# GpSimd's additions wait one VectorE operation earlier, the gating product moves to VectorE, and the second convolution's residual is added from PSUM

## The chip, the cores and the metric

The kernel runs on one core of a Trainium2 chip. The metric is the device time of one execution in microseconds (us), here the median of three runs: 3256.88 us (3255.39 to 3258.67). A difference of about 0.2% (6.5 us) is what the measurement of this kernel can tell from no change.

## The reference, cut to what is computed

Four layers follow each other on an image batch `x` of 4 x 128 channels x 64 x 64.

```
# layer 0: attention over the 4096 pixels, 16-wide queries and keys
attn = softmax(q^T k);  x = gamma * (v attn^T) + x
# layer 1: two 3x3 convolutions with quantised weights, batch norm, 4-bit activations
r  = quant(clip(bn1(conv(x, w1)), 0, 1))          # 15 levels
x  = quant(clip(bn2(conv(r, w2)) + x, 0, 1))      # the residual is added before rounding
# layer 2: a selective scan along the pixels, 256 inner channels, 16 states
xh, z = split(x @ W_in);  xh = silu(causal_conv(xh))
dt, B, C = softplus(...), ...
h[n] = exp(dt * A[n]) * h[n] + dt * B[n] * xh     # a recurrence over 4096 pixels
y  = sum_n h[n] * C[n] + D * xh
y  = y * silu(z)                                  # the gating product
x  = silu(group_norm(y @ W_out)) + x
# layer 3: attention over the pixels, 64-wide; x = x + wo @ agg
```

## The kernel before, in words

Every layer is written as Python generators ("chains"): `energies`, `exponentials` and `products` for the two attentions, `convolutions`, `preparation`, `scans`, `additions`, `output` and so on. Each `yield op(...)` ends a step. The long string `SCORE` has one letter per step (`VOICES` maps letters to chains), and `Order.run` issues the steps in that order. So each engine's program order is written out by hand, across all chains, and is fixed. The costs inside `op(...)` were input to whatever wrote the string and have no effect here; `bank=True` marks a step that takes the one-bank PSUM buffer `gtile` (tag `g`), which a later `release()` gives back.

The pixels of an image are cut into blocks of 512 (the first block of the first image into two of 256), 33 blocks in all. Both halves of the 256 inner channels lie side by side, so a block of one state is 128 partitions x 1024 values. Per block, `preparation` (letter f) makes the inputs, and then for 16 states `m`:

- `scans` (letter n): for every pair of states one VectorE multiplication `hs = ud * b_n` of 2048 values (L1311); for every state two scans of 512 values (L1331), whose decays `da` ScalarE has written to PSUM (L1285); after the next multiplication's scans, `readout` multiplies the pair by `c_n` in place (L1348). On VectorE the steady order is L1311, scan, scan, L1348, scan, scan, L1311 and so on. `hs` has three buffers.
- `additions` (letter o): for every state one GpSimd addition `y += hs` (L1359). After the sixteenth, GpSimd also makes the gating product `y *= sz` (L1363), and `output` (letter g) multiplies by `W_out`.

Which GpSimd operation runs beside which VectorE operation is set by two helpers. `held(inst)` stores the VectorE operation just issued, and `behind(inst)` makes a GpSimd operation wait until the stored one has ended. `held` is put around the VectorE operations that the author calls port operations: L1311, L1348, the four of `preparation` (L1139 to L1148), those of `convolutions` (L938, L950, L977, L984, L987) and L1226. An addition that follows such an operation in the SCORE waits for its end.

The second convolution of `convolutions` (letter e) ends in four steps: ScalarE scales the PSUM bank into an SBUF tile `t` and releases the bank (L973); VectorE adds 15 times the residual image to `t` (L977), clamps it to 0..15 (L984), and rounds it by adding and subtracting a large constant into the FP8 image `x1` (L987).

The attention of the seven first stages runs on TensorE and ScalarE beside the scans. The attention of layer 3 of the last image needs that image's whole layer 2 and runs after the last scan, with VectorE adding the exponentials (L681).

Of the kernel before, what the change touches and what calls it, by code (L numbers as in the profile page):

```python
# [20 lines left out]
P = 128  # L21
W = 64
# [52 lines left out]
    "finish3": "CDEFGHIJ",  # L75
# [4 lines left out]
ittiiuccbvaauitatiaiswjaijaiiukuiviajkajiitkwtiikjijkikcuuisjbbibjkbbittikjjidkikuujiikjibbxcjik  # L80
xxkxbajijabjikkikjjiidxkjayyyykijyieeesejkibjseeiceeceeeekfjkffkijfikffkjjiifdxfjfffxkjxffffpffk
xiixpesfkjkfeffjenlnmlnnfmniinpekfellhmjfnnknenomjoifjkfinhmnlnnmjeifkdlijenpyneylnommjkkihlneyi
eefsnjojknnnflnlhmmffopnnnnfiinkynfkkjiyomlmhjnfpnoonnojlfiknpnjflfmfnonnsmfhkldffnoffkxxnnnxlol
mfppxxnehkfiinenfffejmnnjofekiehlneofmelnjmnnonnikejieneesjflkmeikohjmlnnijpnnijlnophmmnkfflkons
nnodiynijnnyppjmylflfhmkkinjoonnifjfnolflnnnommhnnkfpffkifnnnlnfmhmjokpgonlnnifngjllnfhmfonnnfmn
nikfjffylfmlhpyfmiiokfkdonnonnnnjofkfpfhfknjisljmijfnnonkkploinmnipjjkklnonomnfiikjjhinolkjdfimj
nxnikfxfxxlpnnkxfppjxmoxkkenehenmlijonijeelnmkniijpeeokenhjlnneeeiiemknojnjlfppfnhmkpiodnjinnjfo
kkflkmnnfkflinnmnijhjponppflfmknoniinjogfjklimjgijhnnlkfnokffmndypnpijffnyyfylkkpnyymynflhiejmff
onennokkffijffieejekhkmieelnijnfeenopkinejlmjkndiikjjnloihpneiknjmpnopnklkojpinmfnjikhklnnfomnne
oijflpiknfjkisjfpmdnxjlnmnnoxhpnoiffxjxkkpiljxmiffjnnogklxxmhiisknnojgffkgpennlfefkjifnemopnnejo  # L90
limhiennkjfnpejklnpmfofdiijelnfmkknfnhjoninifjflgnjmnkkijikkjplmpohnifinnonjjkklmnfdijonyffeeffe
ipheenkkjmlnnyykypiiyyojyjffkiijkkknejelopmnnnpmklninhjoiejiipjsdelkjnnompiiknelnhmnffonklnmonnf
fejjkppnfkifpilofmnhnnjjoekflmnzffknnggglpniokotzzzmitudenuxhnelneieeoivmittpfnufuhnmlnpiiwntpit
xxolununxxmfffnflxxmopneheoffffffinnnefeepfelnimtntponeveeesieelomuuniwneefijkhnliifnojjmnijpnln
pkhomiijnneeeejlpkknmnonpkiefelmeeopjnnhfkinijjlmknnkidijmkonlnnfkffsijohljimpnnfjkijkijnoeplenh
pnffmokipljnnoofnfkiimlgnjggkmnknfpnofdyphlnnyfikmfynyoyyjmylpnnonhfnkijjfpfkflmijnonnijlkijkmnn
ophijpkeiiljfkfnmekjonnfpffldmnpoehnnnijiffekifjfpklkjnmnkiikejofnlmphnonnjkiijkjefkofldxnmnijxx
xpnijhlmnkonkiikexjnxxlmonknsijikjjippnlfkjffmennfphijoinlfnmnoefkjlmnhnpopnnofffokidigfkglfmfgp
jnnjhnmfklepoekeiifnnjnpjkelonkimnnpffielojjmkfnffhinijknlonmkdynjeklneepeiyikyyeoyhnmjpnnpyjkif
ylnfoijmkkjneielnihjnkjmiinjjolnmeeeeonnffkfffkpiednppoijjeflkkhnmienenjifkmelpjnokkiijnknjiiljm  # L100
jnhonnklkdmxnpnoijinopjlnkxxxkfmnksxfxpiixhlnnkjmfjofinejnilnjohmnepenoopkfkiiffjlkmffgnkpngeefd
kglnjiiemonhnnepjmoljnkfnfelfkijnfmfnhokifipnnkjipjlmikjfjfkonnnlmfpnfonhkdlnnfeiijmyjeokknlipim
nkpnnojikjhjeenepoilijkjnmnpffiifkffnyyjkyykiydljhmnynkokijifjkklnesjemijonnpnilnmnpfeoekeenpjol
mkiinneknjljepneomkdnxffnepeiijkofxxmfplnxjnkenffxijiopkxxmlknjineljnijpnfkmifonejilkkgmnonnnooj
fgkfmlngeeippnsdelnjmnnpikfoeijfknifjijjfflekkinmonifkfnjklmnnojpffkfnlpiimnonnfjlkndmynjeeioeek
kjlymiyyispenynppkyjjoiikkfjynfffeefnjkfilnjeemneoenkiiljemnkepndkjomlniijhnnpofnkjkilisoenmnjkk
pneofjilmfipjnjhnlnkzfkfmfonnlfpenitkpthimdnxpuxunzxonffiilnvtitxxxiexolzzuumenwimentfitugnounfi
phgngipfgvttfloiggnmniuuoplwffffijnmonghiigjjlnnpknmfnfkoiifeljenmjnnpflhonekepiimfjopnkejlnknii
pkhjmijnjelnonmeeeinoggponffggeffikkfdggkggggggeejglgnjgnkgeeesmgknggeihijkkjlngpgiinokmejknpjlg
nghkpmdnyoiiejjgenijyilkyyykmnegeeynnyfokfijjijkpnkmlnniiheofknjoffjmlnppfinenoijlmknsjfhfnnkoio  # L110
igfdjkjfpmplngkffkgfniglfmhnieefnnjonjiikelekpmoenjnknjlmhoinnpnjifkklfjmopfiidnxnjxnlnmffnjkkox
hfpknpxxxpolmfixnjnijlenphkeomnknijnifjpffkffmiljknknofnpieojeidljhmnnnijeekkkoliijkjmknnnfiflij
jpmhkkeoknnpnildnjmnyioejepnelosypynkiiykyhjmyynkjinijlfkfmjfkffnnpoeeminphoilnkejnffmklnnfjoini
ejlghnjngmnkefoedipnepeoifgslmkfojekknnnpffmeiholjennienkjjemlnfipiojnffkkpnplfhomnjnknieffflkjd
iixnmnonpkjxlxxxnojkxmnxihijjlkefnkkmenonffiifjeeppfjfehknilmknpnionejjijkdlnoijmipnnokkijlifneh
mnnkjjkoeilmeiknkfppnnfjleejsonmnifhniokjjplnfkfmdyinepnijfopljkfyfmkyyhyiinlnfmjnpoyyjneeokgnkk
fgflmgnofhnnfnilimnnjkefpejieiojlmfknnnffhokpnjlmideppiojfkkfjifnnnlnmhjniojlnfmkkiijjkninliksfp
onohmpknnnjjlmokdpnnxfffffnpeikxxxkjijleijmnknhelijoffnexmninkjkijkopnmloijnkhnpnlopkxndmiinxene
jjlnkkiimhnjjkkponepiiflkjknomnenpfjmhfslnnfoknppiijjflkfmfdnynonifljhggmnonnooijikjelyyngyeymne
pikyfyfphlkffnomfnnnelnipofffjmpnjfffehkklnnmenioepneeijlkjnmnoeisijnflkjkidnomhpnneiejjolkfkknm  # L120
nffffkiijefejempepniiplokkhnejnnjezekeflpomknzznnlniimnhvonwliopdxnviminnfwlnfxfimznfhvopenlnfmo
infwxpfifenvhxospmlnnnoofxwlgmingjijpnxxliijgnnmnjhkkkkifofppnikjlkffnmofkipjlfkfnnnhfmnonkfijif
kplnjmokifnnjjkdloidimhjpjennnmelfnkkponkkkknopifjmlhijnfeeijpennfijfflkkkfeokijmnnkkiiddpnjkplj
mehkoiiennnjklpeekknjskmioniCljnhnjiiomnjnfflmnnCkkkokkpjkldpijenifmodhnfnnppjijklomknniienfplkk
fkjmknnhonojklnfiiemknpnjkfjlinhoimnnjppjofkkkfilnmddijnjglengkkkhmnfnonpokfkkflmfpnAiinnjejlehe
mnofnnoijffflmnniiffefkppkjCilkkCChfnCpmnonnooeCkkjjCidCdfgjmklfnnkfffkijijfenhlnkkkminopjepnelo
ikjfCksknDmDniipjkkkenjliioddknjkmpnnpkijlijkjnmkflkiionnmnnjjofkknfplmnnofifjieplnfpfmonnnkjifo
kkojflgfinifpgmkgjfflnmDnonDnnDDDiDjBddilnkkomnDkkklpkmpnojjfnnnfffiljmnifnkkiffoEkEppnjlmonnkkj
pkfflndiijEndikEomjkknknilpEmoEjpiEFjnnnkkkolnFijmnfffjDAffkkinjloiEnEpmfjpnEikknkjiidldmFFkojnn
jnkoklphFmnnnkkiFFiBfjlnFjkkmnFppiiojjlnnkkipjmoinffhknflfnomnkfpjfkdlmhnffioinnnojojlgdgiimnffk  # L130
gppkkjngklggknfpfiomhnjkjnnklnffmiiffnojklkjijmnpfpfFinnAfhofnkkloGGmnnnkddjlnphmofninGGjpplnikk
kkomGkGinGjkjlGmGhijijnnnggpokknfkffkiikfkgjiddlfjkmfHoGnnHnkjlnkoihmpjijnHniiHHkkHHBookflnmpnji
jlgHjmpHnnnohgngkkgggggggpggmgiglkkfkoknnifjfpjggnifidggodlmnfgjkkfnjgkhilgmpnfgpngknoHjfkgkknfo
fiflgfmhnjnifglkgnomjkijfffnlppnmknnionjfkkffpihniddIIlpkmjojIInnhimlnniknpfokjkjnmiiklnfIjnkljk
onphmkkijijnolnniomkppAkkjiIiddIjkknnnlnmnjhfoknpffifIflInijjkkkmnkoiinjjfkklzhmopkknkddnzznittl
noJpiuimulJvinhtInpJtinouuzBiimngJfoJpwntlimtunuJnopnJiolvinmftthniflununpffiomfnwfifjlmnffhngpn
ofglkJnmJijnoffnijlkmhippnnojfijnmknlfffnonijplnhnomnkfkpifjinjfklmiJpjijnkknfdionhlnojippmnjkln
mnkijfionnkjlmikjnknoppffhfnfpijmikjlkfkdnyoinnpijkjijlnikyyyykomynyjiihnkjlefmennjlonmhopkijfkn
neeiienelmjkoppkdijjnnlhmnnokennpkffiiljjonkmffnnpkiljmhionnnpjffikjlmgnfkpfkfnflonmohnnngooikgj
dxffijgmlxikixxxpnkjxknjfxnmlnpipofehjfnneiijkfmpljfinnkojfnfkomlnnfiihnkkjojmlpfdnfnneifffiekkp  # L140
jhmejlfonnneppkiikjijlmjoninneljknkkimikjodnyhlemeneepjenyoyinkyykyijynijkklppnmioneejlhinnjokej
fmfenlpinpneimokjfkffinhnlnojmneijfklnopdmjhnnfifkjnooelnfkfmgkiffigfnmglpkfpenhnnjjlioneeminpjj
kfkfnlonnffpijimnjophneekkldfxonmnfijfnikkxxjiolnmhnixxpknojjlxkxnipimjfnkkfekenlffpfejmeinjlnki
dehjoikffjkknmfenpfopiinneeojlkmihpnnjeiknejjmkipeoljinlnmnknijkjndlhyyyyiioekkmnppyjnjynhloynmk
npofenniijoflkjfpnkmnenifijfjmkpoflhnnijnijfloofkmfnnggkfiihfgdlpkfennjmnfejkeonleomneffflknppni
infkojminjhnoplfinkkjkmnnijliopnfmfnhjplnkdxjnmnoneiexxjliejepekfknoxxkimijxxlenkkeehenfpjffiifk
jkponmnijfnlhmenknijdikofnjlkpijimjennopnlenmkkojheeinnpjmiljpknfonnkiijljkfiknomfnhpjfenedfmyii
lnoknejjyfknfyyyiioyylnppmnkfhnjjelnfmnpofekfgkinglmnniohnffjjmlnnkoepigojieejnelmnfhokfkiniffdj
jefppnlfokfmnnnpkijflnieemkjhfnkiiojneekkejfplffmnkkzzzzndpxiiolvimnxxnnohwfnlviifpxxmownvnnoilp
miwhfnnnivwxxlnpmiiojjiilnnkefkpepnokmnnpolnjjmleeneniikomkjkfkjknnnfifmolnnppejnijlofmnnnoikjkk  # L150
# [37 lines left out]
class Order:  # L188
# [32 lines left out]
    def run(self):  # L221
        for voice in SCORE:
# [7 lines left out]
            if item[1] is None:  # L230
                self.chains.pop(voice)
# [1666 lines left out]
```

## Time and profile before

| what | value |
|---|---|
| median of three runs | 3256.88 us |
| the profiled execution | 3258.73 us |
| its span, first to last instruction | 3256.9 us |
| TensorE busy in the span | 3075.6 us |
| VectorE busy | 2942.3 us |
| ScalarE busy | 2550.4 us |
| GpSimd busy | 1298.7 us |
| mean granted TensorE clock | 0.983 |
| first scan starts, last read-out ends | 104.9 us, 2933.0 us |

The profile has one row per group of instructions (line, engine, operation, shapes, count, busy time, mean duration) and a timeline per engine. Two things help in reading it. A VectorE operation that follows another directly begins, by the record, some 80 ns before the other's recorded end, so the time that one more operation takes up is its duration less 0.08 us. And the duration of an operation holds whatever time it is kept from its operands after its start, so the same operation on the same shape can have different durations; the shortest tenth shows what it takes undisturbed.

### The profile page before, as it was taken

Reading aid. Unit: us, or ns where it says so; the run is one execution under the profiler, and the core shown is the slowest. Engines: PE = TensorE matmul, PEld = TensorE weight load, DVE = VectorE, ACT = ScalarE, POOL = GpSimd, SP = SyncE. Lnnn points to the kernel's source line nnn. Section 1 sums busy time; section 2 is a strip of 40 time slices with the busy share of each in tenths; the row PEclk is TensorE's granted clock in tenths of the full one; section 3 lists DMA queues with packets and bytes.
Section 4 is the critical chain, followed back from the end, with each engine's and each line's share of the span. In section 5 each row is a group of like instructions: output and inputs, shape, how many; then the busy total and the mean of one; then the engine's idle time right before and its main releaser. Section 6 shows DMA issues by size and latency. Waiting matters only on the chain. (4 is left out here: it accounts for less than half of the span.)

```text
span 3256.9 us, 69082 instructions
## 1 busy us (share of the span) xinstructions
PE 3075.6 (94%) x29404; PEld 2260.7 (69%) x29404; DVE 2942.3 (90%) x2377; ACT 2550.4 (78%) x3734; POOL 1298.7 (40%) x582
## 2 busy tenths in 40 slices
PE   8989989999899999999898999999899999999998
PEld 7878858888688887555556878865566555565665
DVE  3699999999999999999999999999999999993554
ACT  5888878888788887888787888878888888875554
POOL 0244444444344444444444444444444444450000
PEclk9999999999999999999999999999999999999999
DMA  2233333233333334333333222233333333330000
GB/s 71 81 99 106 102 118 104 96 108 105 108 117 103 104 102 131 105 109 117 111 130 127 99 98 93 97 125 109 104 125 114 133 114 113 119 108 11 2 11 22
DMA packets 134878, 321.67 MB, mean 99 GB/s; under 512 B 44384, under 2 KB 55072, under 8 KB 134560
## 3 DMA queue, kind: packets, MB, share of 16 engines
q1 hardware_dynamic: 134272, 316.32, 28.9%
q8 instruction: 232, 3.80, 0.5%
q10 hardware_dynamic: 288, 0.85, 0.1%
q14 instruction: 86, 0.70, 0.1%
HBM read 300.35 MB, written 16.78 MB: 97 GB/s over the span
## 5 line engine op out<-in xcount | busy, mean ns | idle before, releaser
L1359 POOL TENSOR_TENSOR y<-y,hs 128x1024 f32<-128x1024 f32 (+1 forms) x528 | 1220.0, 2311 | 1569.1 <-DVE hs L1311 644.6
L659 ACT ACTIVATE p<-e 128x1024 f32<-128x1024 f32 x1024 | 1016.4, 1019 | 183.5 <-PE e L641 161.7
L1331 DVE TENSOR_TENSOR_SCAN hs<-da,hlast,hs 128x512 f32<-128x512 f32 (+1 forms) x928 | 1124.7, 1249 | 36.6 <-ACT da L1285 15.8
L723 PE MATMUL us<-v,p 128*128 128x129 f32 x8192 | 1012.9, 280 | 23.7 <-ACT us L780 11.2
L723 PEld LDWEIGHTS us<-v,p 128*128 128x128 f32 x8192 | 964.5, 194 | 81.4 <-ACT p L659 16.8
L1285 ACT ACTIVATE da<-dt,late 128x512 f32<-128x512 f32 (+1 forms) x1056 | 705.5, 677 | 303.4 <-DVE hs L1331 292.0
L1311 DVE TENSOR_TENSOR hs<-ud,b_n 128x2048 f32<-128x2048 f32 (+1 forms) x264 | 620.0, 2348 | 6.3 <-POOL y L1359 4.2
L1348 DVE TENSOR_TENSOR hs<-hs,c_n 128x2048 f32<-128x2048 f32 (+1 forms) x264 | 590.8, 2238 | 4.5 <-DMA c_n<-bc_d 2.3
L641 PE MATMUL e<-it,v 64*128 64x256 f32 x4096 | 531.6, 396 | 21.7 <-ACT p L659 21.3
L732 PE MATMUL us<-p,v 128*32 128x256 f32 x8192 | 501.8, 383 | 4.7 <-ACT p L659 4.1
L641 PEld LDWEIGHTS e<-it,v 64*128 64x128 f32 x4096 | 373.1, 188 | 162.4 <-issue 74.8
L732 PEld LDWEIGHTS us<-p,v 128*32 128x32 f32 x8192 | 246.2, 110 | 216.5 <-issue 53.3
L641 PE MATMUL e<-it,j 64*128 64x256 f32 x2048 | 208.8, 313 | 24.5 <-ACT p L659 19.3
L641 PEld LDWEIGHTS e<-it,j 64*128 64x128 f32 x2048 | 142.7, 186 | 88.0 <-ACT p L659 31.6
L751 PE MATMUL us<-p,ones 128*32 128x256 f32 x3072 | 202.6, 381 | 0.0
L681 DVE TENSOR_TENSOR acc<-p,acc 128x1024 f32<-128x1024 f32 x96 | 117.5, 1224 | 39.3 <-ACT p L659 32.5
L751 PEld LDWEIGHTS us<-p,ones 128*32 128x32 f32 x3072 | 96.1, 110 | 72.9 <-issue 13.2
L1331 DVE TENSOR_TENSOR_SCAN hs<-da,hs 128x512 f32<-128x512 f32 (+1 forms) x128 | 133.2, 1074 | 7.0 <-ACT da L1285 4.4
L1028 PEld LDWEIGHTS <-w 128*128 128x128 bf16 x594 | 53.1, 98 | 85.8 <-issue 43.9
L1028 PE MATMUL xh<-x,w 128*128 128x512 fp8e4 (+1 forms) x396 | 94.7, 375 | 14.0 <-ACT xc L1074 6.7
L1363 POOL TENSOR_TENSOR y<-y,sz 128x1024 f32<-128x1024 f32 (+1 forms) x33 | 75.9, 2301 | 71.4 <-DVE hs L1348 54.8
L681 DVE TENSOR_TENSOR acc<-p 128x1024 f32<-128x1024 f32 x16 | 19.6, 1224 | 83.1 <-PE ss L694 44.4
(173 smaller groups left out, 2563.6 us busy)
## 6 DMA issues: line engine op xcount, KB each, us to landing
b_n<-bc_d SPq DMA_DIRECT2D x256, 512.0 KB, 3.7
c_n<-bc_d SPq DMA_DIRECT2D x256, 512.0 KB, 3.7
x_in<-in_x SPq DMA_DIRECT2D x16, 512.0 KB, 6.1
xpad<-in_x SPq DMA_DIRECT2D x32, 256.0 KB, 4.6
x_d<-yo SPq DMA_DIRECT2D x24, 256.0 KB, 2.1
x_in<-x_d SPq DMA_DIRECT2D x12, 512.0 KB, 5.1
o<-x_d SPq DMA_DIRECT2D x24, 256.0 KB, 4.0
out<-o SPq DMA_DIRECT2D x24, 256.0 KB, 4.2
```

The source lines that it names most:

```text
L641: nc.tensor.matmul(e[h][:, k % 2, k // 4, :], lhsT=jts[s][row : row + D3, col : col + P], rhs=its[s][row : row + D3, c * CB : (c + 1) * CB ...
L659: nc.scalar.activation(p, es[t][h], AF.Exp)
L681: nc.vector.tensor_add(accs[k], ps[t, h], other)
L723: nc.tensor.matmul(us[:, r, 0:VP], lhsT=ps[t, h][:, k % 2, k // 4, r * P : (r + 1) * P], rhs=vts[s][:, 8 * q + k, :], start=q == 0 and k = ...
L732: nc.tensor.matmul(us[m : m + 32, 0, :], lhsT=vts[s][:, 8 * q + k, m % D3 : m % D3 + 32], rhs=ps[t, h][:, k % 2, k // 4, :], start=q == 0 ...
L751: nc.tensor.matmul(us[32 * m : 32 * m + 32, 1, :], lhsT=ones[:, 0:32], rhs=term, start=False, stop=q == NQ - 1 and k >= len(terms) - 4,)
L1028: nc.tensor.matmul(g, lhsT=w3[:, k // len(rhs), lhs[k % len(rhs)] : lhs[k % len(rhs)] + P], rhs=x[:, rhs[k % len(rhs)]], start=(k == 0), s ...
L1285: nc.scalar.activation(da, live["in", g][0][:, h, :], AF.Exp, scale=amat[:, h, n : n + 1])
L1311: held(nc.vector.tensor_mul(hs, live["in", g][1].unsqueeze(1).to_broadcast([P, 2, 2, T]), bcs.pop(("b", k)).unsqueeze(2).to_broadcast([P, ...
L1331: nc.vector.tensor_tensor_scan(hs[:, m % 2, h, :], das.pop((m, h)), hs[:, m % 2, h, :], hlast[:, n, h : h + 1] if index[g] else 0.0, ALU.mult,
L1348: nc.vector.tensor_mul(hs, hs, bcs.pop(("c", k))[:, a:b].unsqueeze(2).to_broadcast([P, b - a, 2, T]))
L1359: behind(nc.gpsimd.tensor_tensor(y, y, hs[:, m % 2], ALU.add))
```

## The change

Three things are changed, and the whole SCORE is written anew.

1. A new sign `~` in the SCORE marks the next step as early. `held` now stores two operations, the port operation and the VectorE instruction issued just ahead of it. An addition waits for the port operation as before, or, where it is marked `~`, only for the one ahead. 325 of the 528 additions are marked.
2. The gating product is no longer a GpSimd operation behind the sixteenth addition but a chain of its own, `gate` (letter H): for each of the two halves ScalarE copies 512 values of `sz` into the one-bank PSUM buffer, and VectorE multiplies `y` by them and releases the bank.
3. In the second convolution ScalarE scales the PSUM bank in place, VectorE adds the residual from the bank and only then releases it; one VectorE operation does the upper clamp and adds the large constant; ScalarE subtracts the constant and clamps at zero (`Relu`) into `x1`.

```
-    "finish3": "CDEFGHIJ",
+    "finish3": "CDEFG",
+    "gate": "H",
...
-mfppxxnehkfiinenfffejmnnjofekiehlneofmelnjmnnonnikejieneesjflkmeikohjmlnnijpnnijlnophmmnkfflkons
...
+ijijnn~ofyfnknnlfklohmmfifpfijnnonnynnjykpofkflhmlnpfijmfifjn~onnnknfhlmkildnn~onnfnmjxffknixlmx
...
         for voice in SCORE:
+            if voice == "~":
+                self.early = True
+                continue
...
+            self.early = False
...
+    magic = const.tile([P, 1], F32, tag="magic", name="magic")
+    nc.gpsimd.memset(magic, -MAGIC)
...
     def held(inst):
-        holders[:] = [inst]
+        ahead = next(
+            k
+            for k in reversed(nc.cur_bb.bb.instructions)
+            if k is not inst.ins and k.engine == inst.ins.engine
+        )
+        holders[:] = [ahead, inst.ins]
...
     def behind(inst):
-        for holder in holders:
+        for holder in holders[:1] if order.early else holders[1:]:
             tc.add_manual_dep(
...
                 yield op("ACT", 0.2 + 0.58 * part, who=who)
+                nc.scalar.activation(g, g, AF.Identity, bias=b2, scale=s2)
+                yield op("DVE", 0.12 + 0.57 * part, who=who)
                 t = att.tile([P, TB], F32, tag="t", name="q2", bufs=1)[:, 0 : n * W]
-                nc.scalar.activation(t, g, AF.Identity, bias=b2, scale=s2)
+                nc.vector.scalar_tensor_tensor(
+                    img(t), rows_of(xpad, a, n), LEVELS, img(g), ALU.mult, ALU.add
+                )
                 release()
-                yield op("DVE", 0.12 + 0.57 * part, port=True, who=who)
-                held(
-                    nc.vector.scalar_tensor_tensor(
-                        img(t), rows_of(xpad, a, n), LEVELS, img(t), ALU.mult, ALU.add
-                    )
-                )
...
-                held(nc.vector.tensor_scalar(t, t, 0.0, LEVELS, ALU.max, ALU.min))
-                yield op("DVE", 0.1 + 0.33 * part, port=True, who=who)
-                held(
-                    nc.vector.tensor_scalar(
-                        x1s[b % 2][:, 1 + a * W : 1 + (a + n) * W],
-                        t,
-                        MAGIC,
-                        MAGIC,
-                        ALU.add,
-                        ALU.subtract,
-                        saturate=False,
-                    )
+                held(nc.vector.tensor_scalar(t, t, LEVELS, MAGIC, ALU.min, ALU.add))
+                yield op("ACT", 0.2 + 0.49 * part, who=who)
+                nc.scalar.activation(
+                    x1s[b % 2][:, 1 + a * W : 1 + (a + n) * W],
+                    t,
+                    AF.Relu,
+                    bias=magic,
+                    saturate=False,
                 )
...
             if n == DS - 1:
-                yield op("POOL", 0.1 + 2.3 * width(g) / TB, ("sz", g))
-                behind(nc.gpsimd.tensor_tensor(y, y, live.pop(("sz", g)), ALU.mult))
-                mark("gated", g)
+                order.add(gate(g, y))
+
+    def gate(g, y):
+        part = width(g) / TB
+        for h in range(2):
+            yield op("ACT", 0.2 + 0.4 * part, ("sz", g), bank=True)
+            sz = live.pop(("sz", g)) if h == 0 else sz
+            ps = gtile("gate")[:, 0 : width(g)]
+            nc.scalar.copy(ps, sz[:, h, :])
+            yield op("DVE", 0.12 + 0.57 * part)
+            nc.vector.tensor_mul(y[:, h, :], y[:, h, :], ps)
+            release()
+        mark("gated", g)
```

Counted over the whole program, VectorE issues 33 more operations than before (66 products added, 33 roundings gone), ScalarE 99 more (66 copies, 33 `Relu`), GpSimd 33 fewer products and one `memset` more. TensorE's and SyncE's operations are the same in number.

## The prediction, as put on record before the result

> **What bounds the kernel now.** I read the busy table and the 40 slices first:
>
> ```profile
> span 3256.9 us, 69082 instructions
> ...
> PE 3075.6 (94%) x29404; PEld 2260.7 (69%) x29404; DVE 2942.3 (90%) x2377; ACT 2550.4 (78%) x3734; POOL 1298.7 (40%) x582
> ...
> DVE  3699999999999999999999999999999999993554
> ```
>
> TensorE is busiest overall, but VectorE is full from the third slice to the 36th, and the last image's attention (slices 37 to 40) can't begin before its last scan has ended. The printed chain of waits goes back only to 2264 us, so for the rest I go by busy time in the stretch of the scans:
>
> ```profile
> 105.00:2933.00 2828.00, 2668.76 (x24949) 1975.17 (x24951) 2751.02 (x2108) 2316.10 (x3423) 1289.21 (x561) 0.98 0.33 110
> ```
>
> In order: length, then TensorE, weight loads, VectorE, ScalarE and GpSimd. VectorE is idle 77 us of 2828 (19 of them the 104 ns between L1311 and the scan that reads it); TensorE 159. VectorE sets the length; TensorE is second and has room for some 5%.
>
> Is VectorE's busy time all work? The groups by shape, then the timeline:
>
> ```profile
> L1311 DVE TENSOR_TENSOR hs<-ud,b_n 128x2048 f32<-128x2048 f32 x248 | 599.4, 2417 | 6.0 <-POOL y L1359 4.2
> L1348 DVE TENSOR_TENSOR hs<-hs,c_n 128x2048 f32<-128x2048 f32 x248 | 570.1, 2299 | 3.5 <-DMA c_n<-bc_d 2.3 <-ACT hlast L1295 1.2
> ...
> L880 DVE TENSOR_TENSOR o<-o,o 128x512 f32<-128x512 f32 x24 | 16.1, 672 | 2.0 <-PE o L876 2.0
> L987 DVE TENSOR_SCALAR x<-q 128x512 fp8e4<-128x512 f32 x31 | 13.9, 448 | 0.5
> ```
>
> ```profile
> 2341.14 2.27 DVE L1348 TENSOR_TENSOR hs<-hs,c_n 128x2048 f32<-128x2048 f32 x1
> ...
> 2343.32 2.45 DVE L1331 TENSOR_TENSOR_SCAN hs<-da,hlast,hs 128x512 f32<-128x512 f32 x2
> 2343.55 2.36 POOL L1359 TENSOR_TENSOR y<-y,hs 128x1024 f32<-128x1024 f32 x1 [2.37 <-DVE hs L1348]
> ...
> 2345.69 2.37 DVE L1311 TENSOR_TENSOR hs<-ud,b_n 128x2048 f32<-128x2048 f32 x1
> ```
>
> The addition begins 0.14 us after L1348's end and still runs 0.22 us when L1311 begins; that L1311 takes 2.37 us against 2.28 of the shortest tenth. In the next stretch two additions stand behind one port operation, and the next L1311 takes 4.28 us:
>
> ```profile
> 596.14 0.69 DVE L1184 BATCH_NORM_STATS2 stats<-yo 128x6 f32<-128x512 f32 x1
> 596.37 4.87 POOL L1359 TENSOR_TENSOR y<-y,hs 128x1024 f32<-128x1024 f32 x2 [2.45 <-DVE hs L1348]
> 596.75 2.44 DVE L1331 TENSOR_TENSOR_SCAN hs<-da,hlast,hs 128x512 f32<-128x512 f32 x2
> 599.10 4.28 DVE L1311 TENSOR_TENSOR hs<-ud,b_n 128x2048 f32<-128x2048 f32 x1
> ```
>
> So these VectorE operations and a GpSimd addition exclude each other. Measured over the whole timeline against the shortest tenth of each shape: 185 port operations begin with 150 to 400 ns of an addition left and lose 19.4 us; 41 begin with more left (29 of them with over 1 us) and lose 45.3 us. Operations with a PSUM input or scans lose nothing (53 of them begin with over 1 us of an addition left and lose 0.6 us together). **VectorE loses 65 us by standing still behind GpSimd**, and 4.2 us more idle before L1311, waiting for an `hs` buffer.
>
> **The change, part by part.** All sums stand against the profiled execution, 3258.73 us (1.85 above its span and 1.85 above the median).
>
> *VectorE's own work.* Gone: L987, 31 x (0.448 - 0.08) + 2 x 0.22 = 11.9 us. L984 is replaced by one of its own kind and L977 by the same with a PSUM input: 0. New: 62 products of 512 from PSUM, nearest L880 (one PSUM, one SBUF input) at 0.672: 62 x 0.59 = 36.7, and 4 half as long at 0.34: 38.0 us. No row has this product; L977 (two SBUF inputs, 0.686) and L880's shortest (0.657) bound it to 37 and 39. Net **+26.1 us**.
>
> The Trainium skill speaks against going through PSUM: "Perfetto Trace Analysis", section "Optimizing Scalar/DVE Operations", puts VectorE's overhead per instruction at about 60 ns on SBUF and 125 on PSUM. By it (an estimate) 99 operations would cost 6.4 us more. L880 against L977 here shows no such surcharge.
>
> *Early additions.* 325 of 528. What a request does that comes during a port operation is shown twice; one of them:
>
> ```profile
> 2570.71 9.32 POOL L1359 TENSOR_TENSOR y<-y,hs 128x1024 f32<-128x1024 f32 x3 [2.40 <-DVE hs L1311]
> ...
> 2573.11 2.27 DVE L1348 TENSOR_TENSOR hs<-hs,c_n 128x2048 f32<-128x2048 f32 x1
> 2575.29 1.28 DVE L1331 TENSOR_TENSOR_SCAN hs<-da,hlast,hs 128x512 f32<-128x512 f32 x1
> ```
>
> The second of the three additions was requested 46 ns after L1348 began. L1348 was not disturbed (2.27), and the addition ended 2.22 us after L1348's end, where one that waits for the end needs 0.14 + 2.36 = 2.50. That is 0.28 us sooner, and two scans after L1348 last 2.29 from its end to the next start: it fits. So early additions take away the 0.1 us losses. Counted in the new SCORE, 35 unmarked additions still stand behind a read-out with only two scans after it: 35 x 0.105 = 4 us stay. Worth **-15 us**, bounds 0 (the handing over is no faster than the semaphore) and -19.
>
> An early addition could instead come first and hold the port operation up by 2.2 us. Its request needs 0.22 us from the port operation's usual start (0.14 + 0.08). Of 844 port operations 31 started later than that, 24 of them waiting for an addition, and those begin 34 ns after its end while the next addition needs 80. That leaves 7 in 844, or 3 in 325: 6 us at most; I take 0, since the order is new. Behind a waiting addition stand only additions, and behind these L1311 (its buffers) and the gating.
>
> *Gating off GpSimd, L977 no longer exclusive.* GpSimd loses 33 products (75.9 us), and 2 x 33 operations become cover beside which an addition may run. Before, 37 port operations have two additions behind them, which need 4.87 us of cover, mostly with 1.3 to 3.9 there; the new SCORE has 17. By the same loss for each, 45.3 x 17/37 = 20.8 stay: **-24.5 us**, bounds -45 and, if each of the 17 loses a whole 2.2, -8. Waiting of L1311 for buffers: **-3**.
>
> *New waits.* The product waits in VectorE's order for ScalarE's copy and the block's last addition; everything VectorE does is queued behind it. In the new order 2.3 to 10.6 us of VectorE work lie between the last port operation and the first product, except in the last block. Nearest row: L977 waited 1.0 us in all for L973. 66 products at that rate: +2. Bounds: 0 and 66 x 0.69 (a decay or copy of ScalarE in front each time) = 46. The copy waits in ScalarE's order for the bank; behind it are L659 and L1285, whose decays the scans wait for (20 us idle now). ScalarE gets 66 x 0.577 (L1173) + 33 x 0.63 (L952) = 59 us more on 2316 in 2828: **+2** for later decays, bounds 0 and, with the waits doubled, 20. The bank is held some 0.7 us longer per second convolution, 23 us over 33; 2043 us of TensorE's 2669 in the stretch are attention that doesn't use it, so 0, and 23 without that cover. New waits: **+4**.
>
> *At nothing:* the `memset` (GpSimd idles there until 111 us), the DMAs (same in number), the tail (136 exponentials follow the last scan in either order), the last gating (2.35 on GpSimd against 0.67 + 0.58 + 0.67 in turn).
>
> Sum: 26.1 - 15 - 24.5 - 3 + 4 = -12.4, so 3246.3 in a profiled execution, **3244.5 us** by the median.
>
> **Rivals.**
>
> *A, as forecast*, 3236 to 3250. For: VectorE has lost 65 us in known places. Against: two thirds of what is won is spent on the products. 0.47.
>
> *B, nearly all standing still goes:* 26.1 - 69 = -43, or 3214. For: exclusive time falls (GpSimd by 76, L977 and L987 by 35). Against: 17 doubles are still in the SCORE. 0.13.
>
> *C, no difference:* early additions don't begin sooner, or the 17 doubles lose 2.2 each. 26.1 - 0 - 24.5 - 3 + 4 = +2.6 (3259.5), or 26.1 - 15 - 8 - 3 + 4 = +4.1 (3261). 0.17. By the Trainium skill ("SBUF — State Buffer", section "Who interferes with whom") whoever issues first holds the pair for the whole instruction; it gives no time for handing over, so it would leave A and C both open.
>
> *D, slower:* the products wait in VectorE's order for ScalarE's copy. At 0.69 each +46 - 2: 3288. It decides from 12.4/66 = 0.19 us each, and is measurably slower from 0.29. For: ScalarE is 82% busy and takes its copies in order, with one bank. Against: L977 hardly waits today. 0.23.
>
> **The numbers.** Faster by over 0.2% (6.5 us: about what a measurement can tell from no change) are A and B: 0.60; within: C, 0.17; slower: D, 0.23. The range reaches from B's 3215 to 3280, into D, and leaves out about 0.12.
>
> **What would show it.** L1311 by shape falls from 2417 to about 2320 ns, L1348 to 2275; operations over 3 us become half as many; VectorE's idle time before the product's line stays under 5 us; scans end near 2920. The early additions' own records get longer, as they include the port operation. Wrong would be: L1311's mean unchanged (C); idle time before the products <- ScalarE of 20 us and more (D); more idle time of scans <- L1285; TensorE waiting for the bank.

## The result, and the profile after

The changed kernel takes 3218.99 us (median of four runs, 3216.33 to 3222.22) where the kernel before, run beside it, takes 3256.14 (3255.30 to 3258.67). The ratio is 0.9885, 95% interval 0.9868 to 0.9902: **37 us or 1.15% faster**. The direction was forecast, and the time lies in the range, but the gain is three times the forecast 12.4 us. The profiled execution took 3217.55 us, 41 us less than that of the kernel before; the accounts from the traces below are of this one pair of executions.

The busy table and the slices of the kernel after:

```profile
span 3214.9 us, 69188 instructions
...
PE 3047.5 (95%) x29404; PEld 2252.2 (70%) x29404; DVE 2914.6 (91%) x2410; ACT 2600.5 (81%) x3835; POOL 1698.0 (53%) x550
...
DVE  3699999999999999999999999999999999993554
```

The picture is the same, VectorE full from the third slice to the 36th, only shorter. GpSimd's 400 us more are no work: the record of an early addition begins at its request and holds the time for which the port operation keeps it waiting. The stretch of the scans, in the column order given with the prediction:

```profile
105.00:2895.00 2790.00, 2645.26 (x25018) 1968.27 (x25018) 2724.20 (x2144) 2366.25 (x3525) 1695.61 (x531) 0.99 0.34 112
```

From the start of the first scan to the end of the last read-out it was 2828.1 us and is 2781.8. VectorE is idle for 61.3 us of it instead of 77.0. Its groups by shape, after:

```profile
L1324 DVE TENSOR_TENSOR hs<-ud,b_n 128x2048 f32<-128x2048 f32 x248 | 571.9, 2306 | 1.9 <-POOL y L1372 0.2
L1361 DVE TENSOR_TENSOR hs<-hs,c_n 128x2048 f32<-128x2048 f32 x248 | 563.1, 2271 | 0.9 <-DMA c_n<-bc_d 0.9
...
L1385 DVE TENSOR_TENSOR y<-y,gate 128x512 f32<-128x512 f32 x62 | 41.6, 671 | 5.7 <-POOL y L1372 4.4 <-ACT gate L1383 1.1
...
L994 DVE SCALAR_TENSOR_TENSOR q<-xpad,conv 128x512 f32<-128x512 f32 x31 | 20.6, 665 | 0.0
L1001 DVE TENSOR_SCALAR q<-q 128x512 f32<-128x512 f32 x31 | 13.0, 419 | 0.4
```

L1324, L1361 and L1372 are the lines that were L1311, L1348 and L1359. The multiplication went from 2417 to 2306 ns, the read-out from 2299 to 2271, and the idle time ahead of the multiplication from 6.0 to 1.9 us.

**Where the 46.3 us of the stretch come from.** I took the shortest tenth of each shape, over both kernels, as its undisturbed duration. What an operation takes beyond that is its standing still; what is over 60 ns is counted by size.

| VectorE, first scan to last read-out | before | after | difference |
|---|---|---|---|
| undisturbed work (31 more operations, each less 0.08) | | | +23.6 |
| standing still, all | 89.8 | 42.1 | -47.7 |
| of it 60 to 400 ns (159, then 34 operations) | 18.7 | 4.8 | -13.9 |
| of it over 400 ns (34, then 10) | 45.0 | 12.3 | -32.7 |
| idle | 77.0 | 61.3 | -15.7 |
| 80 ns overlaps regained where idle time went | | | -6.5 |

The rest of the standing still (26.1 us before, 25.0 after) is in the scans and in losses under 60 ns. Ahead of the stretch 1.6 us are lost (the first scan starts at 106.5 instead of 104.9) and behind it 2.5 (324 to 326.5), which leaves the 42.0 of the span. The timeline of after shows both kinds of addition:

```profile
1724.06 2.28 DVE L1361 TENSOR_TENSOR hs<-hs,c_n 128x2048 f32<-128x2048 f32 x1
...
1726.26 1.27 DVE L1344 TENSOR_TENSOR_SCAN hs<-da,hlast,hs 128x512 f32<-128x512 f32 x1
...
1726.48 2.35 POOL L1372 TENSOR_TENSOR y<-y,hs 128x1024 f32<-128x1024 f32 x1 [3.79 <-DVE hs L1361]
1727.45 0.72 DVE L547 SCALAR_TENSOR_TENSOR j<-proj,early,h 128x512 fp32r<-128x512 f32 x1
...
1728.10 1.27 DVE L1344 TENSOR_TENSOR_SCAN hs<-da,hlast,hs 128x512 f32<-128x512 f32 x1
...
1729.29 2.26 DVE L1324 TENSOR_TENSOR hs<-ud,b_n 128x2048 f32<-128x2048 f32 x1
...
1729.51 4.26 POOL L1372 TENSOR_TENSOR y<-y,hs 128x1024 f32<-128x1024 f32 x1 [0.68 <-DVE hs L1344]
...
1731.65 2.46 DVE L1344 TENSOR_TENSOR_SCAN hs<-da,hlast,hs 128x512 f32<-128x512 f32 x2
...
1734.03 2.27 DVE L1361 TENSOR_TENSOR hs<-hs,c_n 128x2048 f32<-128x2048 f32 x1
```

The first addition waits for the read-out's end (1726.34), begins 0.14 us later and ends at 1728.83. The new order has put a short operation (L547) between the two scans, so the multiplication begins only at 1729.29, undisturbed. The second addition was asked for 0.22 us after the multiplication had begun. It ends at 1733.77, 2.22 us behind the multiplication's end (1731.55), so two scans are cover enough and the next read-out takes 2.27. By the trace the new SCORE pairs them like this for the most part: other VectorE operations than scans follow 215 of 263 read-outs before the next multiplication or read-out (178 of 263 before), and 185 of the early additions were asked for during a multiplication.

### The profile page after: what moved, and what is told of

The parts are those of the page before. It is cut to its first block, busy times and chain, and to the rows that moved or that the text cites. A ratio compares the mean times of both kernels' runs of the same rounds, so it can differ in the third digit from the quotient of the medians.

```text
span 3214.9 us, 69188 instructions
## 1 busy us (share of the span) xinstructions
PE 3047.5 (95%) x29404; PEld 2252.2 (70%) x29404; DVE 2914.6 (91%) x2410; ACT 2600.5 (81%) x3835; POOL 1698.0 (53%) x550
## 5 line engine op out<-in xcount | busy, mean ns | idle before, releaser
L1372 POOL TENSOR_TENSOR y<-y,hs 128x1024 f32<-128x1024 f32 (+1 forms) x528 | 1695.3, 3211 | 1192.3 <-DVE hs L1361 454.8
L737 PE MATMUL us<-v,p 128*128 128x129 f32 x8192 | 1000.7, 278 | 17.6 <-ACT us L794 10.1
L1324 DVE TENSOR_TENSOR hs<-ud,b_n 128x2048 f32<-128x2048 f32 (+1 forms) x264 | 592.4, 2244 | 3.4 <-POOL y L1372 1.0
L1361 DVE TENSOR_TENSOR hs<-hs,c_n 128x2048 f32<-128x2048 f32 (+1 forms) x264 | 582.4, 2206 | 0.9 <-DMA c_n<-bc_d 0.9
L655 PE MATMUL e<-it,v 64*128 64x256 f32 x4096 | 521.5, 392 | 11.4 <-ACT p L673 11.1
L1131 PE MATMUL dt_ps<-xd,late 128*128 128x256 f32 (+1 forms) x264 | 71.7, 395 | 7.6 <-ACT sp L1143 4.4
```

Of the source, the lines that this page charges most:

```text
L655: nc.tensor.matmul(e[h][:, k % 2, k // 4, :], lhsT=jts[s][row : row + D3, col : col + P], rhs=its[s][row : row + D3, c * CB : (c + 1) * CB ...
L737: nc.tensor.matmul(us[:, r, 0:VP], lhsT=ps[t, h][:, k % 2, k // 4, r * P : (r + 1) * P], rhs=vts[s][:, 8 * q + k, :], start=q == 0 and k = ...
L1324: held(nc.vector.tensor_mul(hs, live["in", g][1].unsqueeze(1).to_broadcast([P, 2, 2, T]), bcs.pop(("b", k)).unsqueeze(2).to_broadcast([P, ...
L1361: nc.vector.tensor_mul(hs, hs, bcs.pop(("c", k))[:, a:b].unsqueeze(2).to_broadcast([P, b - a, 2, T]))
L1372: behind(nc.gpsimd.tensor_tensor(y, y, hs[:, m % 2], ALU.add))
```

## The experiments

**Theory:** VectorE sets the end, it loses 65 us standing still behind GpSimd, and each of the three parts takes some of that away. **Rivals:** the early request does nothing; the gain is the written order's and not the parts'; gating or the convolution's tail only pays for itself. Ratios are to the kernel before, measured beside each run; by their intervals the difference of two runs of the table is uncertain by some 6 to 8 us.

| run | what it is | median us | ratio, 95% interval |
|---|---|---|---|
| x1_no_early | after, no addition early | 3233.31 | 0.9920 (0.9904, 0.9937) |
| x4_gate_gpsimd | after, gating on GpSimd | 3241.42 | 0.9947 (0.9931, 0.9964) |
| x5_conv_old | after, the tail of before | 3249.17 | 0.9968 (0.9956, 0.9981) |
| x6_gate_sbuf | after, product from SBUF | 3233.24 | 0.9921 (0.9904, 0.9939) |
| x8_old_work | new order, all three undone | 3283.09 | 1.0074 (1.0057, 1.0091) |
| x3_tiny_after | after, GpSimd's work cut away | 3203.10 | 0.9830 (0.9813, 0.9846) |
| x2_tiny_before | before, GpSimd's work cut away | 3195.34 | 0.9800 (0.9784, 0.9817) |
| x7_before_early | before, every GpSimd operation early | 3232.01 | 0.9912 (0.9895, 0.9928) |
| y1_conv_before | before, new tail | 3297.60 | 1.0118 (1.0102, 1.0133) |
| y2_conv_early | before, new tail and all early | 3278.99 | 1.0058 (1.0044, 1.0072) |
| y5_gate_conv_early | as y2, gating on VectorE too | 3362.64 | 1.0316 (1.0302, 1.0331) |
| y3_all_early | after, all 528 additions early | 3211.74 | 0.9861 (0.9846, 0.9876) |

**How much is there to win? (x2, x3)** Both cut GpSimd's additions to 4 of 512 columns, x2 its gating product as well.

```
-            behind(nc.gpsimd.tensor_tensor(y, y, hs[:, m % 2], ALU.add))
+            behind(nc.gpsimd.tensor_tensor(y[:, :, 0:4], y[:, :, 0:4], hs[:, m % 2, :, 0:4], ALU.add))
```

> The kernel before with GpSimd's additions and products cut to 4 of 512 columns of each half, so that what GpSimd computes is left out but for these; all waits and orders stay. Theory (VectorE's standing still behind GpSimd is 64 us and 5 us of waiting for buffers, and VectorE sets the length): 3256 - 69 = 3187. Rival (TensorE, busy for 94%, takes over as soon as VectorE gets faster): less than half of it, 3220 or more.

> The changed kernel with GpSimd's additions cut to 4 of 512 columns of each half, the rest of them left out. Theory: what still stands still there, 17 us, and 1 us of waiting for buffers goes: 3219 - 18 = 3201. Rival (there is far more hidden exclusion, or TensorE is the bound): 3190 or less, or no change at 3219.

The groups of before with GpSimd cut away:

```profile
L1311 DVE TENSOR_TENSOR hs<-ud,b_n 128x2048 f32<-128x2048 f32 x248 | 563.8, 2273 | 1.6 <-DMA b_n<-bc_d 0.2
L1348 DVE TENSOR_TENSOR hs<-hs,c_n 128x2048 f32<-128x2048 f32 x248 | 562.7, 2269 | 2.0 <-DMA c_n<-bc_d 1.9
```

No operation stands still for over 60 ns any more, and the kernel before becomes 64 us faster (2.0% of 3259.36). In the kernel after the same cut wins only some 18 us by the ratios (16 by the medians). That VectorE's standing still was worth about 64 us, and that some 18 are left, is shown; the two numbers also agree with the 63.7 and 17.1 us found in the traces.

**Early additions alone, both ways (x1, x7)**

```
-        for holder in holders[:1] if order.early else holders[1:]:
+        for holder in holders[1:]:
```

That is x1. In x7 the kernel before gets the new `held`, and every GpSimd operation is early:

```
-        holders[:] = [inst]
...
+        holders[:] = [ahead, inst.ins]
...
-        for holder in holders:
+        for holder in holders[:1]:
```

> The changed kernel with every addition waiting for the port operation itself; the sign for early additions is read and ignored, the order is the same. Theory (early additions end 0.28 us sooner, which matters where only two scans follow): of the 325 marked additions 192 stand behind L1324, whose two scans give 2.48 us for 2.50, so 192 x 0.02 = 4 us; the other 133 stand behind operations with 2.29 us of cover and lose 0.1 us each, 13 us: 17 us slower than the changed kernel, 3236. Rival (the new order alone gives the gain, the handing over is worth nothing): within 3 us of 3219. Rival (early additions are the whole gain): back to 3256.

> The kernel before, order and all, with every GpSimd operation waiting only for the VectorE operation ahead of the port operation. Additions that need the read-out they stand behind can't gain, since their data comes no sooner. Theory: the 85 or so others with 2.29 us of cover lose 0.1 us less each (8 us), and the second of two additions behind one operation ends 0.28 us sooner at 37 places (9 us): 3256 - 17 = 3239. Rival (the early request takes the port ahead of the VectorE operation): 2.2 us at each such place, 3270 or more. Rival (nothing without the new order): 3250 to 3260.

The multiplication in x1, then in x7:

```profile
L1324 DVE TENSOR_TENSOR hs<-ud,b_n 128x2048 f32<-128x2048 f32 x248 | 577.4, 2328 | 4.4 <-POOL y L1372 2.3
```

```profile
L1316 DVE TENSOR_TENSOR hs<-ud,b_n 128x2048 f32<-128x2048 f32 x248 | 585.6, 2361 | 1.6
```

In the new order the marks are worth 0.35% (11 us): standing still of 60 to 400 ns goes from 15.5 to 4.8 us and the idle time for buffers from 3.6 to 1.0. In the old order, with nothing else changed, they are worth 28.7 us; there operations that stood still for 60 to 400 ns fell from 159 to 54 and the wait for `hs` buffers went. In x7 some 400 additions were asked for during a port operation; their median end is 2.22 us after its end. The rivals that a request buys nothing, and that it takes the port ahead of the VectorE operation, fall. I had expected 17 us in both; the size in either order was wrong by some 6 to 12 us.

**Gating back on GpSimd, or from SBUF (x4, x6).** Both leave ScalarE's copies out. In x4 GpSimd makes the product at the place of the first half's copy, in x6 VectorE multiplies all 1024 values from SBUF at the place of the first half's product. x4, then x6:

```
-            sz = live.pop(("sz", g)) if h == 0 else sz
-            ps = gtile("gate")[:, 0 : width(g)]
-            nc.scalar.copy(ps, sz[:, h, :])
+            if h == 0:
+                behind(nc.gpsimd.tensor_tensor(y, y, live.pop(("sz", g)), ALU.mult))
...
-            nc.vector.tensor_mul(y[:, h, :], y[:, h, :], ps)
```

```
-            ps = gtile("gate")[:, 0 : width(g)]
-            nc.scalar.copy(ps, sz[:, h, :])
...
-            nc.vector.tensor_mul(y[:, h, :], y[:, h, :], ps)
+            if h == 0:
+                nc.vector.tensor_mul(y, y, live.pop(("sz", g)))
```

> The changed kernel with the gating product back on GpSimd, as one operation behind the last port operation at the place of the first copy; copies and VectorE's 66 products are gone, the order is otherwise the same. Theory (the product on GpSimd costs VectorE more, by standing still, than its own two products): VectorE's own work falls by 37 us, and 33 products of 2.36 us look for cover that is given to additions, at some 1.4 us each 46 us: about 3228, and operations over 3 us on VectorE become some 30 more. Rival (moving the product cost more than it gave): 3210 or less.

> The changed kernel with the gating product on VectorE as one operation of 1024 values from SBUF at the place of the first product; the 66 copies to PSUM are left out. Theory (what the way through PSUM buys is that the product may run beside an addition): own work the same (33 x 1.14 against 66 x 0.59), but the product waits for an addition under way, or makes one wait: additions run some 44% of the time, so about 15 of 33 lose 1.2 us, 18 us slower than the changed kernel, 3237. Rival (the detour through PSUM buys nothing, and ScalarE's 38 us and the bank come free): 3219 or less.

VectorE's two large groups in x4, and the product in x6:

```profile
L1361 DVE TENSOR_TENSOR hs<-hs,c_n 128x2048 f32<-128x2048 f32 x248 | 600.9, 2423 | 1.5 <-DMA c_n<-bc_d 0.9 <-ACT hlast L1308 0.5
L1324 DVE TENSOR_TENSOR hs<-ud,b_n 128x2048 f32<-128x2048 f32 x248 | 586.2, 2364 | 4.9 <-POOL y L1372 2.3 <-DMA b_n<-bc_d 0.8
```

```profile
L1383 DVE TENSOR_TENSOR y<-y,sz 128x1024 f32<-128x1024 f32 x31 | 50.7, 1637 | 4.4 <-POOL y L1372 4.4
```

In x4 VectorE is rid of 36.8 us of products, but its read-outs take 37.8 us more and its multiplications 14.3: 34 operations stand still for a microsecond or more (62.1 us) against 7 (10.2) in after. Net 20 us lost, where I expected 9. In x6 some of the products themselves stand still: the median of all 33 is 1.22 us, close to the undisturbed 1.20, but the mean of the 31 full ones is 1.64 and the longest takes 3.40. So what the detour through PSUM buys is not a cheaper product (two halves take 2 x 0.59 = 1.18 in turn, one whole 1.14) but one that doesn't exclude an addition. It costs ScalarE 37.8 us of copies and saves 12 us of the end, where 18 were expected.

**The convolution's tail (x5), and the new order alone (x8).** x5 puts back the tail of before in the new order (the rounding stands where the `Relu` stood), but without `held` around the residual and the rounding, so that no addition is made to wait for them:

```
-                nc.scalar.activation(g, g, AF.Identity, bias=b2, scale=s2)
...
+                nc.scalar.activation(t, g, AF.Identity, bias=b2, scale=s2)
...
-                    img(t), rows_of(xpad, a, n), LEVELS, img(g), ALU.mult, ALU.add
+                    img(t), rows_of(xpad, a, n), LEVELS, img(t), ALU.mult, ALU.add
...
-                held(nc.vector.tensor_scalar(t, t, LEVELS, MAGIC, ALU.min, ALU.add))
+                held(nc.vector.tensor_scalar(t, t, 0.0, LEVELS, ALU.max, ALU.min))
...
-                nc.scalar.activation(
+                nc.vector.tensor_scalar(
```

x8 is the edits of x1, x4 and x5 together.

> The changed kernel with the end of the second convolution as it was: ScalarE scales into SBUF, VectorE adds the residual from SBUF, clamps, and rounds in an operation of its own at the place of the Relu; the order is otherwise the same, and the new order left no gaps of GpSimd for the two SBUF operations. Theory: VectorE's own work +13 us; the 66 operations that exclude additions again stand beside additions in the new order, 0.7 and 0.45 us long, and lose some 10 us: 23 us slower than the changed kernel, 3242. Rival (VectorE's own work alone counts): +13, 3232. Rival (ScalarE's 21 us less make up for it): 3222 or less.

> The new order with all three parts undone: additions wait for the port operation, the gating product is on GpSimd, the second convolution ends as before. Theory (the order was written for the three parts and gives nothing by itself): the losses of the single undoings add up, 11 + 22 + 20 = 53 us over the changed kernel, 3270, slower than before. Rival (a better order is the gain): 3219 to 3235.

The residual and the rounding in x5, then the two large groups in x8:

```profile
L994 DVE SCALAR_TENSOR_TENSOR q<-xpad,q 128x512 f32<-128x512 f32 x31 | 28.9, 933 | 0.0
L1003 DVE TENSOR_SCALAR x<-q 128x512 fp8e4<-128x512 f32 x31 | 28.1, 905 | 0.1
```

```profile
L1326 DVE TENSOR_TENSOR hs<-ud,b_n 128x2048 f32<-128x2048 f32 x248 | 594.4, 2397 | 8.8 <-POOL y L1374 6.7
L1363 DVE TENSOR_TENSOR hs<-hs,c_n 128x2048 f32<-128x2048 f32 x248 | 594.1, 2396 | 1.4 <-DMA c_n<-bc_d 0.9 <-ACT hlast L1310 0.5
```

The new order counts the residual as cover for an addition. With the second operand in SBUF it takes 933 ns, from PSUM (L994 of after) 665. The Trainium skill ("SBUF — State Buffer", section "Who interferes with whom") states that VectorE contends with a GpSimd instruction that reads SBUF when it has two SBUF inputs, and outside its two-port modes not with at most one; the residual's two rows agree. The rounding, with one SBUF input, was kept waiting too (905 ns against 448 in the kernel before, L987); the page leaves that open only for the two-port modes, and no run here shows in which mode it ran. x5 costs 27 us by the ratios where 23 were expected; in its profiled execution VectorE's own work is 11 us more than in after, its standing still 22 more and its idle time 3 less.

Undone one at a time the parts cost 11 (early), 20 (gating) and 27 us (tail), together 58; undone all at once they cost 61. So in the new order they add, within what these runs can tell. But x8 is 24 us **slower** than the kernel before: the new order without the new work is a bad order, with 96.8 us of standing still instead of 63.7. (Here too the residual and the rounding are without `held`, so part of that may be additions that `held` would have kept away.) The 61 us are more than the 37 that the whole change gains, so undoing a part in an order made for it doesn't tell what that part is worth by itself: the early requests are worth more in the old order (28.7 us, with all of them early), and the tail, as the next runs show, less.

**New work in the old order (y1, y2, y5).** y1 is the new tail in the order of before; y2 adds the edit of x7; y5 adds the product on VectorE as well. The edit of y1, then what y5 adds:

```
-                nc.scalar.activation(t, g, AF.Identity, bias=b2, scale=s2)
-                release()
-                yield op("DVE", 0.12 + 0.57 * part, port=True, who=who)
...
+                nc.scalar.activation(g, g, AF.Identity, bias=b2, scale=s2)
...
+                nc.vector.scalar_tensor_tensor(
+                    img(t), rows_of(xpad, a, n), LEVELS, img(g), ALU.mult, ALU.add
                 )
+                release()
+                yield op("DVE", 0.12 + 0.57 * part, who=who)
...
+                yield op("ACT", 0.2 + 0.49 * part, who=who)
+                nc.scalar.activation(
```

```
+    def flush(now=True):
+        for p in list(pending):
+            p[0] -= 1
+            if now or p[0] <= 0:
+                pending.remove(p)
+                nc.vector.tensor_mul(p[1], p[1], p[2])
...
-                behind(nc.gpsimd.tensor_tensor(y, y, live.pop(("sz", g)), ALU.mult))
+                pending.append([4, y, live.pop(("sz", g))])
```

> The kernel before with the new tail of the second convolution alone (residual from PSUM, one VectorE operation for the upper clamp, ScalarE's Relu); order and additions as before. The residual is issued right behind ScalarE's scaling, as the bank can't be kept over other steps of this order. Theory (parts add up, whatever the order): 12.5 us of VectorE's own work go, and of the 63.7 us of standing still some 5 to 15, as 66 of 844 port operations no longer exclude an addition: 17 to 28 us faster, about 3237, ratio 0.995 to 0.991. Rival (the 27 us that this part was worth in the new order came from an order written for it): only the 12.5 us, less up to 33 x 0.4 = 13 us for a VectorE that now waits right behind ScalarE's scaling: 0 to 12 us faster, 0.996 to 1.000.

> The kernel before, its order kept, with the new convolution tail and with every addition and product of GpSimd asked for one VectorE operation early; gating stays on GpSimd. Theory (the parts take away different losses and add): 28.7 us of the early additions and 17 to 28 of the tail, 46 to 57 us faster: 3200 to 3211, ratio 0.986 to 0.9825, so faster than the change as made (0.9885). Rival (both take away the same losses, or the early requests do so only where two scans follow): 35 us or less, 0.989 or more.

> All three parts on the order of before: as the run with tail and early additions, and the gating product on VectorE, but from SBUF, one operation of 1024 values per block, issued four scan steps behind the last addition and without ScalarE's copies. Theory (what gating wins is standing still of VectorE behind GpSimd, of which tail and early additions leave some 25 us): 33 x 1.1 = 36 us of new VectorE work against at most 25 us won, so 5 to 20 us slower than that run, 3215 to 3230. Rival (the product's exclusive 76 us on GpSimd cost as much here as in the new order, where undoing the gating cost 20 us and the SBUF form 12): 8 us faster than that run.

Theory and rival both missed y1, y2 and y5 (103 us slower than before): the tail in the old order makes the kernel 38 us slower instead of up to 28 faster. ScalarE's waits in y1, then VectorE's, then the scans' in before (in us, times, longest):

```profile
ACT x L986 <- DVE q L984: 43.2, 17, 4.8
```

```profile
DVE hs L1327 <- ACT da L1281: 36.8, 43, 3.2
...
DVE q L976 <- ACT conv L974: 8.5, 8, 2.6
```

```profile
DVE hs L1331 <- ACT da L1285: 20.3, 29, 1.7
```

The `Relu` (L986) waits in ScalarE's order for VectorE's clamp, 43.2 us in all, up to 4.8 at once, and everything behind it, the decays among it, comes late: the scans wait 36.8 us for them instead of 20.3. VectorE's undisturbed work falls, its idle time rises from 77.0 to 128.3 us. Another 8.5 us are the residual's wait for ScalarE's scaling, which y1 issues right ahead of it. These two make up half of the 51 us more idle time; most of the rest are other waits for ScalarE, each longer than before. That the `Relu`'s wait is behind them is argued: no run moves the `Relu` alone. The same `Relu` row in the kernel after:

```profile
ACT x L1003 <- DVE q L1001: 7.6, 9, 1.7
```

With the `Relu` at a place that the new order gave it, the same wait is 7.6 us. y2 wins back 0.6% by early requests but stays slower than before. In y5 the SBUF product stands in VectorE's order four scan steps behind the last addition and ScalarE's next `sz` must wait for it:

```profile
ACT sz L1054 <- DVE y L1364: 95.6, 28, 5.1
```

Here the `sz` buffer is held longer and the product stands still in 20 of 33 cases by over 0.4 us. That place was my choice, so y5 doesn't tell what gating is worth in the old order; this stays open.

**All additions early (y3)**

```
-        for holder in holders[:1] if order.early else holders[1:]:
+        for holder in holders[:1]:
```

> The changed kernel with all 528 additions early and not only 325. Theory (an early request never comes in front of the port operation, and ends 0.28 us sooner): at most the 4.8 us of small losses go, 3214 to 3219, ratio 0.987 to 0.9885. Rival (the 203 were left unmarked because an early request there would come first and hold the port operation up): a tenth of them at 2.2 us is 45 us, 3264, 1.002; even 10 such cases would make it 22 us slower.

The rival falls: no port operation is held up by the 203 others. The ratio is 0.24% lower than that of after, but the intervals overlap, so whether this version beats the changed kernel isn't settled; it is not slower by anything that could be seen. Standing still is the same within 0.5 us. Some of the unmarked additions can't be early anyway: an addition behind a read-out reads what it writes. In y3 172 additions still start within 0.2 us behind a read-out's end (median 0.14 us), where 179 do in after; behind 26 of them a VectorE operation stands still for over 60 ns, 4.4 us in all, where in after it is 29 and 4.5.

## Why the prediction was right in direction and a third in size

**What bounds the kernel: right.** VectorE's standing still was put at 65 us; cutting GpSimd's work away wins 64.

**VectorE's own work, +26.1: right, +23.6.** The product took 671 ns (shortest 657) where L880's 672 was taken. The residual from PSUM took 665 where 686 was costed at no difference. The page's rule of a dearer PSUM access ("Perfetto Trace Analysis", section "Optimizing Scalar/DVE Operations"), 6.4 us by its figures, isn't seen in either row.

**Early additions, -15: right in mechanism, and in size with the order's help.** Small losses fell by 13.9 us, and 4.8 stayed where 4 were said to stay, at the place named: 28 of the 34 are behind an addition that began 0.14 us after a read-out's end. The step "ended 2.22 us after L1348's end", read from two cases, held for 309 (2.225 in the middle, 2.216 to 2.245 from the tenth to the ninetieth hundredth). That an early addition never comes first, costed at 0 with a bound of 6, is what y3 shows even for all 528. The 13.9 are the sum with the order: without the marks 15.5 us of small losses are left in the new order (x1), so the marks take away 10.7 of them. By the time the marks alone are worth 11 in the new order and 28.7 (all additions and products) in the old.

**Gating off GpSimd, L977 no longer exclusive, -24.5: right kind, 8 too little.** Losses over 400 ns fell by 32.7. The step that was mis-sized is "By the same loss for each, 45.3 x 17/37 = 20.8 stay": 12.3 stay, in 10 operations instead of 17, so some of the doubles counted in the new SCORE seem to have had enough cover; no run counts them. Only three operations (not scans) take over 3 us instead of 18, where half was forecast.

**Waits, -3 and +4: the step that failed.** The prediction's "Waiting of L1311 for buffers: -3" and "New waits: +4" let every other wait stand as it was. VectorE's idle time with the overlaps that go with it fell by 22 us instead of rising by one. By the waits: attention's `it` waiting for ScalarE 6.0 to 0.9, `hs` for GpSimd 4.2 to 1.0, the read-outs for ScalarE's `hlast` copy 2.2 to below 0.5, the others in single microseconds. Two of these rows, before and after:

```profile
DVE it L533 <- ACT h L531: 6.0, 3, 3.1
DVE hs L1311 <- POOL y L1359: 4.2, 24, 0.3
```

```profile
DVE hs L1324 <- POOL y L1372: 1.0, 2, 0.8
...
DVE it L547 <- ACT h L545: 0.9, 1, 0.9
```

What changed them is mostly the rewritten order: in x8, with none of the new work, attention's wait is 1.8 already, and all idle time but the wait of `hs` for GpSimd is 61.2 instead of 72.8; with early requests that wait goes too (x1 3.6, after 1.0). The products waited 1.1 us for ScalarE's copies, 0.02 each, against the 0.19 from which rival D would have decided, and 4.4 once in the last block. The scans' wait for decays went from 20.3 to 19.1 where +2 was costed.

These three differences (23 for the waits, 8 for the large losses, 2.5 for own work) are the 34 us by which the stretch was shortened more than forecast. That the time still lies in the range is owed to the range's width: its lower end is rival B's 3215.

**The rivals.** C falls by x1 and x7, and by the 12.3 us that the large losses still cost, where it takes 37. B's time, 3214, is the nearest, but its reason is only partly met: 17 us of standing still remain (x3 puts them at 18), and the rest of B's gain came from waits. D didn't happen at the gating. Its mechanism, a ScalarE step and a VectorE step waiting for each other in fixed orders, is real, though: in y1 the `Relu` waits 43.2 us for the clamp and the kernel gets 38 us slower, and the prediction hadn't costed this wait at all. In the changed kernel it is 7.6 us, with the `Relu` at a place of the new order; the prediction looked at that order for the additions and the products, not for the `Relu` and not for the waits that were there already.

## What to carry to other kernels

Where every engine's order is written by hand, price an edit together with its order: the convolution's tail is worth 27 us in an order made for it and costs 38 in the other. List the waits between engines that the edit creates (here `Relu` on the clamp) and look in the new order for what stands between the two; then list the waits that the new order no longer has. When an operation stands still behind another engine, cutting that engine's work to a sliver and keeping its waits, as in x2, measures in one run what that standing still costs in the given order.

## What the runs showed of the hardware that was not expected

- An addition that is asked for while VectorE's port operation runs ends 2.22 us after that operation's end; one that waits for the end on a semaphore ends 2.50 us after it (0.14 until its start, then 2.35). The 0.28 us between them are more than the semaphore's 0.14, so the queued addition needs some 0.13 us less than its 2.35 once the operands come free. In reverse it is much the same: the 25 VectorE operations of the kernel before that lost over 0.8 us ended 0.11 to 0.15 us sooner after the addition's end than their undisturbed duration. What saves this time, the traces don't show.
- The record of GpSimd counts such waiting as busy: its busy time is 1698.0 us with 325 early additions and 1217.9 with none (x1), for the same work.
- The 104 ns between the multiplication and the scan that reads it stay in every version: 206 to 223 times, 21.4 to 23.2 us in sum (23.0 in the kernel before, where the prediction has 19).
